# Layer 0 in two halves, one continuous dense stream, and a gated product of one ACT copy and three POOL products

## The chip, the cores and the metric

The kernel runs on one core of a Trainium2 chip. Its time is the device time in microseconds of one execution. Engines are named as the profile names them: PE multiplies matrices (PEld is its weight load), DVE, ACT and POOL work element by element, and SP issues most transfers. Each engine works through its own queue in order and waits at semaphores for the others. `V`, `S`, `G` and `T` in the code are DVE, ACT, POOL and PE.

## The reference, cut to what matters

All arrays are float32. Four batches of 512 tokens with 256 features pass two layers.

```python
xn = layernorm(x)                                     # layer 0
q, k, v = xn @ Wq.T + bq, xn @ Wk.T + bk, xn @ Wv.T + bv
context = (elu(q) + 1) * cumsum((elu(k) + 1) * v, axis=1) * 0.25
attn = context @ Wo.T + bo
xr = rms(xn) * norm_w                                 # and the gene part
vals, idx = top_k((xr @ Wc.T) / clip(temperature), 32)      # of 512
e = einsum(softmax(vals), genes[idx])
x = x + attn + tanh(e @ Wd.T) * xr * (e @ Wu.T) * scale

xn = layernorm(x)                                     # layer 1
q, k, v = split(rms(xn) @ w_qkv.T); w = exp(rms(k))
y = sigmoid(rms(q)) * cumsum(w * v) / (cumsum(w) + 1e-6)
u, g = split(y @ w_swiglu.T)                          # 2 x 1024 columns
dense = xn + (u * silu(g)) @ w_out.T
# 16 experts, the best 2 of each token (inner width 176), and a shared
# expert of inner width 352 that every token passes
x = x + dense + moe(xn) + shared_expert(xn)
```

## The kernel before

The tokens lie on the partitions in 16 tiles of 128, four to a batch; `xs` holds x throughout. Python generators describe pieces of work, `yield` marks places where another piece may come in, and `together` interleaves several generators in proportion to how far each has come. A tile scheduler then decides the final order within each engine's queue; tile pools with few buffers make a piece wait until an earlier user is done.

- `layer0(b, i0, nt)` does layer 0 for nt tiles: `statistics` (mean `mv`, inverse deviations `rs`; `sl` at L232 scales the logits), `normalise` (L213, one DVE instruction for a tile), transposes (L221), the logits (L289), the search for the 32 best of 512 (`top`: four rounds of an eight-fold maximum, L301, and a replacement, L302, on DVE, then the exponential L307), the linear attention (`attend_kv`, `attend_q`: projections L244, `phi` L257 to L259, a running sum L271 on DVE, the product with q into `ctxT` L280 on DVE with the factor 0.25 as `QSCALE`), the gene part (`express`, L316 to L334, whose last steps are POOL's `dn` and `xs` products) and the output projection (`out`, L339).
- `mix(b, i0, nt)` is layer 1 up to `yT`: statistics and `normalise` again, xs plus xn1 on POOL (L368), the w1 projections (L384), the copy of q and k (L391, ACT), the scaling of v (L393, DVE), squares (L396), roots, exponentials (L410, L411), the product with v on POOL (L412), transposes and running sums (L421), the reciprocal (L430), `yT` (L432), and the choice of experts (L439 to L456).
- `dense(b, half, busy)` takes 256 tokens through 11 chunks of 128 hidden columns, three of the shared expert (input `xn1T`) and eight of the swiglu (input `yT`). A chunk is an "up" (eight matmuls into the PSUM tile `gu`, L578), a tanh (L582, ACT), a gated product, and a "down" (four matmuls, L595, added up in `acc`) that comes two chunks later. `gu` has three buffers, `acc` one. Each half runs its own last two downs out before the next half's first up, and ends with acc added to xs (L614).
- `route`, `scatter`, the expert loop (pairs of 128-row groups: L738, L747, L759) and the final part: the gather of each token's two expert rows (L804, POOL) and their addition to xs (L815, DVE). `pr` (L486) is the first matmul of `route`.

The gated product of a chunk is

```python
V.scalar_tensor_tensor(th[0:m], th[0:m], 1.0, gu[0:m, 0], ALU.add, ALU.mult)
if busy:
    S.copy(hid[0:m], gu[0:m, 1])
    G.tensor_tensor(hid[0:m], hid[0:m], th[0:m], ALU.mult)
else:
    V.tensor_tensor(hid[0:m], gu[0:m, 1], th[0:m], ALU.mult)
```

with `busy` true for the four halves of batches 0 and 1, that is 44 of the 88 chunks. The order is: layer 0 of the first two tiles; mixing of these beside layer 0 of the other two; then the mixing of one batch, layer 0 of the next and one dense half together, three times; the mixing of batch 3 with the last half of batch 1, in which the expert weights are fetched into `wex` (after a memset of part of it on POOL); then routing and scattering beside 22 chunks of batch 2; the experts; and batch 3's 22 chunks beside the gathers and final additions. `paced` ties some transfers to the dense chunks' downs.

Of the kernel before, what the change touches and what calls it, by code (L numbers as in the profile page):

```python
# [11 lines left out]
F32 = mybir.dt.float32  # L12
# [4 lines left out]
P = 128  # L17
B, L, D = 4, 512, 256
NT = L // P
# [34 lines left out]
def tile_two_layers(  # L54
# [79 lines left out]
    nc.sync.dma_start(wot, wo0.rearrange("(h p) e -> p h e", p=P))  # L134

# [12 lines left out]
    for b in range(1, B):  # L148
        load_x(b)
# [5 lines left out]
    for h in range(NH):  # L155
        V.tensor_scalar(wct[:, h], wct[:, h], nwc[:, h : h + 1], None, ALU.mult)
    rtemp = wp.tile([P, 1], F32, name="rtemp")
# [28 lines left out]
    one = first.enter_context(tc.tile_pool(name="one0", bufs=1, side="right"))  # L186
# [7 lines left out]
    def statistics(pool, b, i0, nt):  # L194

        mv = pool.tile([P, NT, 2], F32, name="mv")
        rs = pool.tile([P, 2, NT], F32, name="rs")
        ve = pool.tile([P, NT], F32, name="ve")
        for i in range(nt):
            bs = pool.tile([P, 6], F32, name="bs")  # L200
            V.bn_stats(bs, xs[:, b, i0 + i])
            V.bn_aggr(mv[:, i], bs)
        V.tensor_scalar(rs[:, 0, 0:nt], mv[:, 0:nt, 1], LN_EPS, None, ALU.add)
        V.reciprocal(ve[:, 0:nt], rs[:, 0, 0:nt])
        V.tensor_tensor(ve[:, 0:nt], ve[:, 0:nt], mv[:, 0:nt, 1], ALU.mult)
        V.tensor_scalar(rs[:, 1, 0:nt], ve[:, 0:nt], RMS_EPS, None, ALU.add)
        S.activation(rs[:, :, 0:nt], rs[:, :, 0:nt], AF.Sqrt)
        V.reciprocal(rs[:, :, 0:nt], rs[:, :, 0:nt])
        return mv, rs

    def normalise(to, b, i0, nt, mv, rs):
        for i in range(nt):
            V.tensor_scalar(  # L213
                to[:, i], xs[:, b, i0 + i], mv[:, i, 0:1], rs[:, 0, i : i + 1], ALU.subtract, ALU.mult
            )
# [8 lines left out]
    def layer0(b, i0, nt):  # L224

        W = nt * P
        mv, rs = statistics(io, b, i0, nt)
        xn = io.tile([P, NT, D], F32, name="xn")
        normalise(xn, b, i0, nt, mv, rs)

        sl = io.tile([P, 2, NT], F32, name="sl")
        V.tensor_scalar(sl[:, 0, 0:nt], rs[:, 1, 0:nt], rtemp, None, ALU.mult)  # L232
        V.tensor_scalar(sl[:, 1, 0:nt], rs[:, 1, 0:nt], scl, None, ALU.mult)
        yield
        xnT = io.tile([P, NH, L], F32, name="xnT")
        for h in range(NH):
            S.copy(xnT[:, h, 0:W], turn(xn, nt, h * P))  # L237
        yield


        def project(c):
            pm = bank()[:, 0:W]
            for h in range(NH):
                T.matmul(  # L244
                    pm,
                    wqkv[:, h, c * P : (c + 1) * P],
                    xnT[:, h, 0:W],
                    start=(h == 0),
                    stop=(h == NH - 1),
                )  # L250
            return pm

        def phi(c):

            pm = project(c)
            e = io.tile([P, L], F32, name="phi", bufs=3)[:, 0:W]
            S.activation(e, pm, AF.Relu, bias=nbqk[:, c : c + 1], scale=-1.0)  # L257
            S.activation(e, e, AF.Exp, scale=-1.0)
            V.scalar_tensor_tensor(e, pm, bqkv1[:, c : c + 1], e, ALU.add, ALU.max)  # L259
            return e  # L260

        ctxT = one.tile([P, NH, L], F32, name="ctxT")
        cums = {}

        def attend_kv(h):
            fk = phi(2 + h)
            pv = project(4 + h)
            kv = one.tile([P, L], F32, name="kv")[:, 0:W]
            V.scalar_tensor_tensor(kv, pv, bqkv[:, 4 + h : 5 + h], fk, ALU.add, ALU.mult)
            cum = io.tile([P, L], F32, name="cum")[:, 0:W]  # L270
            V.tensor_tensor_scan(  # L271
                cum, ones[:, 0:W], kv, carry[:, h : h + 1] if i0 else 0.0, ALU.mult, ALU.add
            )
            if i0 + nt < NT:
                V.tensor_copy(carry[:, h : h + 1], cum[:, W - 1 : W])
            cums[h] = cum

        def attend_q(h):
            fq = phi(h)
            V.scalar_tensor_tensor(ctxT[:, h, 0:W], fq, QSCALE, cums[h], ALU.mult, ALU.mult)  # L280


        rden = io.tile([P, NT], F32, name="rden")
        exT = one.tile([P, L], F32, name="exT")

        def logits(i):
            pl = bank()
            for h in range(NH):
                T.matmul(  # L289
                    pl, xnT[:, h, i * P : (i + 1) * P], wct[:, h], start=(h == 0), stop=(h == NH - 1)  # L290
                )
            lg = io.tile([P, NG], F32, name="lg")
            S.copy(lg, pl)
            return lg

        def top(i, lg):
            tp = io.tile([P, NACT], F32, name="top")
            rep = io.tile([P, NG], F32, name="rep")
            for r in range(NACT // 8):
# [3 lines left out]
                if r == 0:  # L303
                    nm = io.tile([P, 1], F32, name="nm")
                    V.tensor_scalar(nm, tp[:, 0:1], sl[:, 0, i : i + 1], -1.0, ALU.mult, ALU.mult)
                    e = io.tile([P, NG], F32, name="e")
                    S.activation(e, lg, AF.Exp, bias=nm, scale=sl[:, 0, i : i + 1])  # L307
            den = io.tile([P, 1], F32, name="den")
            V.scalar_tensor_tensor(e, rep, TAKEN, e, ALU.is_equal, ALU.mult, accum_out=den)
            V.reciprocal(rden[:, i : i + 1], den)  # L310
            return e

        def express(i, e):
# [8 lines left out]
            S.copy(exT[:, i * P : (i + 1) * P], px[:, 0:P])  # L322
            du = bank()
            T.matmul(du, exT[:, i * P : (i + 1) * P], wdut, start=True, stop=True)  # L324
# [8 lines left out]
            G.tensor_tensor(xs[:, b, i0 + i], xs[:, b, i0 + i], bob, ALU.add)  # L333
            G.tensor_tensor(xs[:, b, i0 + i], xs[:, b, i0 + i], dn, ALU.add)  # L334

        def out(i):
# [5 lines left out]
            V.tensor_tensor(xs[:, b, i0 + i], ao, xs[:, b, i0 + i], ALU.add)  # L342


        parts = [lambda h=h, f=f: f(h) for h in range(NH) for f in (attend_kv, attend_q)]
        lg = logits(0)
        for i in range(nt):
            nxt = logits(i + 1) if i + 1 < nt else None
            e = top(i, lg)
            yield  # L350
            for part in parts[i * len(parts) // nt : (i + 1) * len(parts) // nt]:
                part()
            yield
            express(i, e)
            lg = nxt
            yield
        for i in range(nt):
            out(i)
            yield

    def mix(b, i0, nt):
# [17 lines left out]
        for i in range(nt):  # L379
# [13 lines left out]
            V.tensor_scalar(vs[:, i], pv[:, 0:D], rs[:, 1, i : i + 1], None, ALU.mult)  # L393
            for j in range(2):
                junk = w2.tile([P, D], F32, name="junk")
# [170 lines left out]
    def dense(b, half, busy):  # L566


        unit = (b, 2 * half) if (b, 2 * half) in made else (b, 0)
        t0 = (2 * half - unit[1]) * P  # L570
        ins = [a[:, :, t0 : t0 + HB] for a in made[unit]]
        acc = ps_a.tile([P, 2, D], F32, name="acc")

        def up(gw, g0, uw, u0, m, which, dw, dc):
# [6 lines left out]
            th = wd.tile([P, HB], F32, name="th", bufs=3)  # L581
            S.activation(th[0:m], gu[0:m, 0], AF.Tanh, scale=0.5)  # L582
            hid = wd.tile([P, HB], F32, name="hid", bufs=4)
            V.scalar_tensor_tensor(th[0:m], th[0:m], 1.0, gu[0:m, 0], ALU.add, ALU.mult)  # L584
            if busy:
                S.copy(hid[0:m], gu[0:m, 1])  # L586
                G.tensor_tensor(hid[0:m], hid[0:m], th[0:m], ALU.mult)  # L587
            else:
                V.tensor_tensor(hid[0:m], gu[0:m, 1], th[0:m], ALU.mult)  # L589
            return hid  # L590

        def down(n, hid):
            m, dw, dc = chunks[n][4], chunks[n][6], chunks[n][7]
            for t in range(2):
# [8 lines left out]
            beat.append(mm.ins.name)  # L603

        hids = []
        for n, c in enumerate(chunks):
            hids.append(up(*c))
            if n >= 2:
                down(n - 2, hids[n - 2])
            yield  # L610
        for n in (NC - 2, NC - 1):
            down(n, hids[n])
        here = xs[:, b, 2 * half : 2 * half + 2]
        V.tensor_tensor(here, acc, here, ALU.add)  # L614
        yield


    def chain(*parts):
        for part in parts:
            yield from part  # L620

    H = NC + 1

    def a(b, i0, nt):
        return layer0(b, i0, nt), 2 + 4 * nt

    def m(b, i0, nt):
        return mix(b, i0, nt), 6 + nt

    def d(b, half, busy=True):  # L630
        return dense(b, half, busy), H

    together(a(0, 0, 2))
    together(m(0, 0, 2), a(0, 2, 2))
# [5 lines left out]
    together(m(0, 2, 2), a(1, 0, 4), d(0, 0))  # L640
    together(m(1, 0, 4), a(2, 0, 4), d(0, 1))
    together(m(2, 0, 4), a(3, 0, 4), d(1, 0))
# [27 lines left out]
    together(m(3, 0, 4), d(1, 1), (load_experts(), 17))  # L670
    mixing.close()
    routing = ctx.enter_context(ExitStack())
    d2 = chain(dense(2, 0, False), dense(2, 1, False))
    together((route(), 8), (islice(d2, 6), 6))
    routing.close()

    together((scatter(), 33), (islice(d2, 15), 15))
    run_all(d2)
# [121 lines left out]
    for step, _ in enumerate(chain(dense(3, 0, False), dense(3, 1, False))):  # L800
# [11 lines left out]
        while added < 2 * NTT and 9 * added <= 16 * (step - 4):  # L812
# [61 lines left out]
```

## Time and profile before

| | |
|---|---|
| median of 10 runs | 591.61 us (589.47 to 593.33) |
| profiled execution, its own time | 592.26 us |
| its span, first to last instruction | 590.6 us |
| mean granted TensorE clock | 0.978 |
| busy: PE, DVE, ACT, POOL | 540.4, 375.1, 233.1, 171.9 us |
| busy share: PE, DVE, ACT, POOL | 92%, 64%, 39%, 29% |
| all transfers | 47.39 MB |

The profile names a group of instructions by line, engine, operation, and output and input tiles with their shape; after the bar stand the busy time in us and the mean of one in ns, then the idle time of the engine just before these instructions and what ended it. The rows of slices show 40 equal stretches of the span with the busy share of each engine in tenths. The table by stretches has, for each window, its bounds and length, each engine's busy time with the count of instructions in the order PE, PEld, DVE, ACT, POOL, and then the granted clock, the share of DMA and its rate in GB/s. The chain of waits follows the work that ended last back to the start; a row has the start in us, the length in us, the engine, tile and line. Matmuls are pipelined and their ends are modelled, so a busy PE is not always at its full pace.

### The profile page before, as it was taken

The page shows a single profiled execution, that of the slowest core. Times are in us where ns is not written, and L with a number is a line of the kernel's source. Part 1 is how long each engine was busy: PE and PEld are TensorE (multiplying, and loading weights), DVE is VectorE, ACT ScalarE, POOL GpSimd, SP SyncE. Part 2 cuts the span into 40 slices and gives each one's busy share as a digit, 9 for nine tenths or more (in the row PEclk, how much of TensorE's full clock was granted, in tenths as well). Part 3 has the DMA queues.
Part 4 walks back from the last instruction along what each step waited for, and adds up shares of the span by engine and source line. Part 5 has one row for each costly group of instructions (what it writes and reads, how often), then busy time and mean ns, then how long its engine had stood idle before and what let it go on. Part 6 is the DMA issues. An engine that isn't in the chain of part 4 may idle for free.

```text
span 590.6 us, 7339 instructions
## 1 busy us (share of the span) xinstructions
PE 540.4 (92%) x2384; PEld 393.9 (67%) x2384; DVE 375.1 (64%) x992; ACT 233.1 (39%) x528; POOL 171.9 (29%) x214
## 2 busy tenths in 40 slices
PE   3557989989999999999999999979999999999897
PEld 1333556567565776567767778866777777788686
DVE  3979999998796897968953795323222222235553
ACT  1453846652655716457155411112333333321011
POOL 1234232343222523224250325661000000016660
PEclk9788999999999999999999999989999999999899
DMA  5993000000000000000065702224333333124440
GB/s 160 374 376 139 1 1 0 2 0 1 1 1 0 0 2 1 1 1 0 2 187 156 233 13 71 96 83 142 94 105 105 108 108 98 55 68 129 125 143 28
DMA packets 38453, 47.39 MB, mean 80 GB/s; under 512 B 4016, under 2 KB 34960, under 8 KB 38160
## 3 DMA queue, kind: packets, MB, share of 16 engines
q1 hardware_dynamic: 35344, 38.53, 20.1%
q0 software_dynamic: 3072, 8.39, 4.6%
q8 instruction: 20, 0.33, 0.2%
q14 instruction: 17, 0.14, 0.1%
HBM read 28.30 MB, written 18.61 MB: 79 GB/s over the span
## 4 chain that ended last, share of the span: by engine, by line
PE 62%; DVE 24%; ACT 5%; issue 5%; POOL 2%; DMA 1%; SPq 0%; ACTq 0%; DVEq 0%
PE gu L578 17%; PE acc L595 10%; PE pu L738 9%; PE py L759 7%; PE pm L384 5%; PE pt L701 4%; DVE rep L302 3%; DVE top L301 3%; PE pm L244 3%; DVE sums L430 3%; PE pm L289 3%; DVE sums L421 2%; PE pm L324 2%; DVE xn L213 1%; PE pm L221 1%
## 5 line engine op out<-in xcount | busy, mean ns | idle before, releaser
L578 PE MATMUL gu<-yT,wugt 128*128 128x256 f32 x512 | 126.2, 383 | 0.0
L578 PEld LDWEIGHTS gu<-yT,wugt 128*128 128x128 f32 x512 | 95.8, 191 | 19.8 <-issue 7.4
L582 ACT ACTIVATE th<-gu 128x256 f32<-128x256 f32 (+1 forms) x88 | 33.2, 382 | 129.6 <-PE gu L578 88.6
L595 PE MATMUL acc<-wot,hid 128*128 128x256 f32 x256 | 68.1, 392 | 8.9 <-DVE hid L589 6.1
L804 POOL DMA_INDIRECT ys<-yrows,slot x32 | 30.5, 953 | 143.1 <-DMA yrows<-yg 127.6
L584 DVE SCALAR_TENSOR_TENSOR th<-th,gu 128x256 f32<-128x256 f32 (+1 forms) x88 | 36.0, 411 | 51.1 <-ACT th L582 28.9
L738 PE MATMUL pu<-wex,xgT 128*128 x188 | 63.8, 461 | 0.8 <-ACT xgT L715 0.8
L595 PEld LDWEIGHTS acc<-wot,hid 128*128 128x128 f32 x256 | 48.6, 194 | 20.8 <-DVE hid L589 7.7
L587 POOL TENSOR_TENSOR hid<-hid,th 128x256 f32<-128x256 f32 (+1 forms) x44 | 33.7, 769 | 95.7 <-ACT hid L586 95.6
L244 PE MATMUL pm<-xnT,wqkv 128*128 128x512 f32 (+1 forms) x120 | 46.4, 527 | 4.5 <-ACT qk L391 1.7
L747 DVE TENSOR_TENSOR hb<-pu,hb 128x176 f32<-128x176 f32 x47 | 16.1, 342 | 51.0 <-ACT hb L746 51.0
L578 PE MATMUL gu<-xn1T,sgu 128*128 128x256 f32 (+1 forms) x192 | 45.9, 384 | 0.0
L384 PE MATMUL pm<-w,xn1T 128*128 128x512 f32 (+1 forms) x128 | 44.8, 493 | 0.6 <-DVE vs L393 0.6
L759 PE MATMUL py<-wex,hgT 128*128 x188 | 44.5, 379 | 0.0
L759 PEld LDWEIGHTS py<-wex,hgT 128*128 128x128 f32 x188 | 35.6, 190 | 8.6 <-issue 0.2
L578 PEld LDWEIGHTS gu<-xn1T,sgu 128*128 128x128 f32 (+1 forms) x192 | 34.7, 184 | 7.0 <-issue 0.9
L738 PEld LDWEIGHTS pu<-wex,xgT 128*128 128x128 f32 x188 | 32.0, 190 | 11.0 <-ACT xgT L715 1.0
L384 PEld LDWEIGHTS pm<-w,xn1T 128*128 128x128 f32 x128 | 24.2, 190 | 22.2 <-issue 17.7
L244 PEld LDWEIGHTS pm<-xnT,wqkv 128*128 128x128 f32 x120 | 23.8, 201 | 22.3 <-issue 13.9
L751 DVE COPY hgT<-pt 128x512 f32<-128x512 f32 (+1 forms) x24 | 16.3, 681 | 34.3 <-PE pt L701 34.3
L544 POOL DMA_INDIRECT xrows<-xn,slot x32 | 30.9, 966 | 23.1 <-DVE cpair L538 9.7
L289 PE MATMUL pm<-wct,xnT 128*128 128x512 f32 x64 | 33.7, 666 | 0.3 <-ACT xnT L237 0.2
(162 smaller groups left out, 880.6 us busy)
## 6 DMA issues: line engine op xcount, KB each, us to landing
xrows<-zero SPq DMA_DIRECT2D x1, 6016.0 KB, 22.6
xg<-xrows SPq DMA_DIRECT2D x23, 256.0 KB, 4.2
yrows<-yg SPq DMA_DIRECT2D x23, 256.0 KB, 2.1
wex<-in_w_gate_up_dram SPq DMA_DIRECT2D x8, 704.0 KB
xs<-in_x_dram SPq DMA_DIRECT2D x4, 512.0 KB
wugt<-in_wug_dram SPq DMA_DIRECT2D x1, 2048.0 KB, 12.1
wex<-in_w_down_dram SPq DMA_DIRECT2D x4, 512.0 KB
out_dram<-xs SPq DMA_DIRECT2D x7, 256.0 KB, 2.8
```

Of the source, the lines that this page charges most:

```text
L244: T.matmul(pm, wqkv[:, h, c * P : (c + 1) * P], xnT[:, h, 0:W], start=(h == 0), stop=(h == NH - 1),)
L289: T.matmul(pl, xnT[:, h, i * P : (i + 1) * P], wct[:, h], start=(h == 0), stop=(h == NH - 1))
L384: T.matmul(o[:, 0:n], xnT[:, h, i * P : (i + 1) * P], w1[:, h, at : at + n], start=(h == 0), stop=(h == NH - 1),)
L544: sc = G.indirect_dma_start(out=xrows, out_offset=bass.IndirectOffsetOnAxis(ap=slot[:, k, i : i + 1], axis=0), in_=xn1[:, i // NT, i % NT] ...
L578: T.matmul(gu[0:m, k], w[:, h, at : at + m], ins[which][:, h], start=(h == 0), stop=(h == NH - 1))
L582: S.activation(th[0:m], gu[0:m, 0], AF.Tanh, scale=0.5)
L584: V.scalar_tensor_tensor(th[0:m], th[0:m], 1.0, gu[0:m, 0], ALU.add, ALU.mult)
L587: G.tensor_tensor(hid[0:m], hid[0:m], th[0:m], ALU.mult)
L595: mm = T.matmul(acc[:, t], hid[0:m, t * P : (t + 1) * P], dw[0:m, dc], start=(n == 0 and t == 0), stop=(n == NC - 1), skip_group_check=True,)
L738: T.matmul(pg[:, 0 : 2 * NI], xT[:, i, h], wex[:, bass.ds(at[i] + h * 2 * NI, 2 * NI)], start=(h == 0), stop=(h == NH - 1),)
L759: mm = T.matmul(py[:, i * D : (i + 1) * D], hT[:, i, h], wex[:, bass.ds(at[i] + EW - (2 - h) * D, D)], start=(h == 0), stop=(h == 1),)
L804: G.indirect_dma_start(out=ys[:, asked], out_offset=None, in_=yrows, in_offset=bass.IndirectOffsetOnAxis(ap=slot[:, k, n : n + 1], axis=0) ...
```

## The change

Layer 0 is split into `front` (statistics, normalising, transposes, the four tiles' logits and the attention, always for a whole batch) and `back` (search, gene part and output projection for nt tiles). In `front` the product into `ctxT` is made by POOL; the factor 0.25 goes into `wot` once, by an ACT instruction. For batches 0 and 1 (`wide`) the projections use the PSUM tiles of the dense part. `normalise` and the scaling of v become ACT instructions; for that, `statistics` gets one more small DVE instruction, which forms minus mean times inverse deviation. The logits' exponential is written in place and `lg` has five buffers.

`dense` becomes one stream of 88 chunks through all eight halves, in which downs stay two chunks behind across the meeting of two halves; `islice(dd, n)` takes the next n. While `calm` is empty (all mixing) a chunk's product is made without DVE: an ACT copy of both halves of `gu`, and three POOL products, gate·up, tanh times that, and the sum. From `route` on, DVE makes the product as it did before. `th` has two buffers instead of three, `junk` one instead of two. 40 chunks lie in the mixing now, 26 in routing and scattering, 22 at the end. The order of work is written anew, x of batch 1 is fetched ahead of the layer 1 weights, and the final additions follow the chunks by another rule.

```diff
+    load_x(1)
     w1 = const.tile([P, NH, 3 * D + NE], F32, name="w1")
...
+    S.mul(wot, wot, QSCALE)
...
         V.reciprocal(rs[:, :, 0:nt], rs[:, :, 0:nt])
+        V.scalar_tensor_tensor(mv[:, 0:nt, 0], mv[:, 0:nt, 0], -1.0, rs[:, 0, 0:nt], ALU.mult, ALU.mult)
...
-            V.tensor_scalar(
-                to[:, i], xs[:, b, i0 + i], mv[:, i, 0:1], rs[:, 0, i : i + 1], ALU.subtract, ALU.mult
+            S.activation(
+                to[:, i], xs[:, b, i0 + i], AF.Identity, bias=mv[:, i, 0:1], scale=rs[:, 0, i : i + 1]
             )
...
-    def layer0(b, i0, nt):
+    def front(b, wide):
...
         def project(c):
-            pm = bank()[:, 0:W]
+            if wide:
+                pm = ps_d.tile([P, 2, HB], F32, name="gu").rearrange("p i c -> p (i c)")
+            else:
+                pm = bank()
...
-            V.scalar_tensor_tensor(ctxT[:, h, 0:W], fq, QSCALE, cums[h], ALU.mult, ALU.mult)
+            G.tensor_tensor(ctxT[:, h], fq, cums[h], ALU.mult)
...
+        for h in range(NH):
+            for i in (2 * h, 2 * h + 1):
+                logits(i)
+                yield
+            attend_kv(h)
+            yield
+            attend_q(h)
+            yield
+
+    def back(b, i0, nt):
...
+        top(i0)
+        yield
+        for i in range(i0, i0 + nt):
+            if i + 1 < i0 + nt:
+                top(i + 1)
+                yield
+            express(i)
             yield
-        for i in range(nt):
+        for i in range(i0, i0 + nt):
             out(i)
             yield
...
-            V.tensor_scalar(vs[:, i], pv[:, 0:D], rs[:, 1, i : i + 1], None, ALU.mult)
+            S.activation(vs[:, i], pv[:, 0:D], AF.Identity, scale=rs[:, 1, i : i + 1])
...
-            th = wd.tile([P, HB], F32, name="th", bufs=3)
+            th = wd.tile([P, HB], F32, name="th", bufs=2)
             S.activation(th[0:m], gu[0:m, 0], AF.Tanh, scale=0.5)
             hid = wd.tile([P, HB], F32, name="hid", bufs=4)
-            V.scalar_tensor_tensor(th[0:m], th[0:m], 1.0, gu[0:m, 0], ALU.add, ALU.mult)
-            if busy:
-                S.copy(hid[0:m], gu[0:m, 1])
-                G.tensor_tensor(hid[0:m], hid[0:m], th[0:m], ALU.mult)
+            if spare:
+                V.scalar_tensor_tensor(th[0:m], th[0:m], 1.0, gu[0:m, 0], ALU.add, ALU.mult)
+                V.tensor_tensor(hid[0:m], gu[0:m, 1], th[0:m], ALU.mult)
             else:
-                V.tensor_tensor(hid[0:m], gu[0:m, 1], th[0:m], ALU.mult)
+                both = w2.tile([P, 2, HB], F32, name="both")
+                S.copy(both[0:m], gu[0:m])
+                G.tensor_tensor(hid[0:m], both[0:m, 0], both[0:m, 1], ALU.mult)
+                G.tensor_tensor(th[0:m], th[0:m], hid[0:m], ALU.mult)
+                G.tensor_tensor(hid[0:m], hid[0:m], th[0:m], ALU.add)
...
+        behind = []
+        for half in range(2 * B):
...
+            for n, c in enumerate(chunks):
+                behind.append((half, n, up(ins, bool(calm), *c)))
+                if len(behind) > 2:
+                    down(*behind.pop(0))
+                yield
...
+    f0, f1 = front(0, True), front(1, True)
+    b0 = back(0, 0, 2)
+    run_all(islice(f0, 4))
+    together(some(f0, 6), some(b0, 2))
+    together(some(b0, 4), some(f1, 2))
+    m0 = mix(0, 0, 2)
+    next(m0)
+    run_all(islice(f1, 3))
+    together((m0, 7), some(f1, 5))
...
-    together(m(0, 2, 2), a(1, 0, 4), d(0, 0))
-    together(m(1, 0, 4), a(2, 0, 4), d(0, 1))
-    together(m(2, 0, 4), a(3, 0, 4), d(1, 0))
+    together((back(0, 2, 2), 6), d(3))
+    m0 = mix(0, 2, 2)
+    next(m0)
+    run_all(islice(dd, 2))
+    together((m0, 7), d(3))
+    together((back(1, 0, NT), 12), (front(2, False), 10), d(9))
+    m1 = mix(1, 0, NT)
+    next(m1)
+    run_all(islice(dd, 2))
+    together((m1, 9), (back(2, 0, NT), 12), (front(3, False), 10), d(3))
+    m2 = mix(2, 0, NT)
+    next(m2)
+    run_all(islice(dd, 2))
+    together((m2, 9), (back(3, 0, NT), 12), d(9))
...
-    together(m(3, 0, 4), d(1, 1), (load_experts(), 17))
+    m3 = mix(3, 0, NT)
+    next(m3)
+    run_all(islice(dd, 2))
+    together((m3, 9), d(5), (load_experts(), 17))
...
-    together((route(), 8), (islice(d2, 6), 6))
+    calm.append(True)
+    together((route(), 8), d(5))
...
-    together((scatter(), 33), (islice(d2, 15), 15))
-    run_all(d2)
+    together((scatter(), 33), d(15))
+
+    run_all(islice(dd, 6))
...
-        while added < 2 * NTT and 9 * added <= 16 * (step - 4):
+        while added < 2 * NTT and 17 * added <= 32 * (step - 3):
```

## The prediction, made before the changed kernel was run

> **What bounds the kernel now.** I read the page's slices first, then the table by stretches, the chain of waits for the pace of the matmuls, the groups by form for prices, and last who waits for whom.
>
> From the page, tenths of 40 slices of 14.8 us:
>
> ```profile
> PE   3557989989999999999999999979999999999897
> DVE  3979999998796897968953795323222222235553
> PEclk9788999999999999999999999989999999999899
> ```
>
> PE is full from slice 6 on; DVE is full before that and nearly full until slice 19; the clock is granted in part only where PE starves. The table by stretches (length, then busy time of PE, PEld, DVE, ACT, POOL):
>
> ```profile
> 0.00:80.00 80.00, 50.86 (x193) 30.70 (x194) 65.83 (x210) 35.92 (x79) 21.62 (x37) 0.89 0.56 194
> 80.00:140.00 60.00, 56.81 (x243) 36.02 (x244) 58.16 (x161) 32.38 (x69) 23.68 (x33) 1.00 0.00 1
> 140.00:220.00 80.00, 78.04 (x343) 53.37 (x341) 66.27 (x165) 40.87 (x92) 23.96 (x30) 1.00 0.00 1
> 220.00:290.00 70.00, 67.78 (x294) 44.45 (x294) 58.16 (x155) 39.12 (x87) 21.80 (x26) 1.00 0.00 1
> 346.00:406.00 60.00, 55.65 (x248) 47.21 (x246) 26.04 (x69) 7.67 (x20) 32.67 (x37) 0.97 0.23 78
> ```
>
> Matmuls overlap, so busy time flatters PE. The chain of waits shows their real pace where nothing holds them:
>
> ```profile
> 169.11 1.72 PE pm L289 x4
> 170.83 2.63 PE pm L384 x8
> 414.69 1.73 PE py L759 x8
> 419.67 1.73 PE py L759 x8
> 531.08 1.73 PE gu L578 x8
> 533.67 1.73 PE gu L578 x8
> ```
>
> A 512-column matmul (two records) takes 0.86 us, a dense chunk 2.59 (up 1.73, down 0.86), an expert pair 4.97. So 88 chunks are 228 us, 23.5 pairs 117, layer 0 of a batch 28.5 (logits 6.9, projections 10.4, expression 6.9, out 3.5, transposes 0.9; four times 114), the mixing of a batch 14.0 (56 in all): 515 us. The span is 590.6, so PE loses 75. Counting records at that pace by stretch, the losses are 41 (to 80 us), 5 (to 140), 8 (to 290), 3 (to 346), 8 (to 406), 1 (experts), 9 (end, of it 4 at 550 to 557 where two halves of the dense part meet, and 4 to 5 of tail). The PE work is the same matmuls in both kernels; only these 75 us can move.
>
> **The change, part by part.** Prices, from the groups by form (mean ns after the comma):
>
> ```profile
> L584 DVE SCALAR_TENSOR_TENSOR th<-th,gu 128x256 f32<-128x256 f32 x80 | 32.8, 412 | 48.7 <-ACT th L582 27.4 <-issue 21.1
> L587 POOL TENSOR_TENSOR hid<-hid,th 128x256 f32<-128x256 f32 x40 | 30.8, 774 | 86.1 <-ACT hid L586 86.1
> L586 ACT COPY hid<-gu 128x256 f32<-128x256 f32 x40 | 14.9, 372 | 35.7 <-DVE th L584 35.5
> L391 ACT COPY qk<-pm 128x512 f32<-128x512 f32 x16 | 9.3, 582 | 20.2 <-PE pm L384 20.2
> L213 DVE TENSOR_SCALAR xn<-xs,mv,rs 128x256 f32<-128x256 f32 x32 | 15.2, 526 | 0.2
> ```
>
> *DVE.* Leaves: the dense product, 44 of L584 (18.1 us); 32 normalisations (16.8); 16 of L393 (476 ns, 7.6); ten ctxT products (5.8); the doubled fixed cost of batch 0's halves (about 2). Comes: ten small products of mv (0.2 each, 2). Some 48 us less.
>
> *ACT.* The dense copy goes from 372 to 582 ns (same shape as L391): 40 times 0.21 is 8.4 us. A normalisation with two pointer operands has no row: without pointers a 256-wide pass from SBUF takes 413 (L258), with one 509 (L410), and two pointers add 185 at 512 wide (L307's 813 against 628); so 0.41 to 0.60, and I take 0.55, as it has two: 17.6 us. The vs product has a like row, 473 (L326): 7.6. The listing of the changed kernel's ACT queue has 29 table loads where 23 stood, at 1283 each: 7.7. Together 41 us; ACT goes from 53% of 80 to 290 to about two thirds.
>
> *POOL.* A chunk goes from one product to three. Its row has median 727, mean 774: 40 times 1.5 is 60 us, and eight ctxT products at about 1.33 (L368, 512 wide) add 11. POOL goes from 33% to some 60%.
>
> *The start.* Both listings have the same searches (32 MAX8, 32 replacements) in DVE's queue between the first MAX8 and the last yT of batch 0. By row means the items between sum to 137.0 us before and 114.7 after; before, they took 125.2 (15.3 to 140.5). At that ratio, 0.914, they take 105 after. The first MAX8 comes some 2 us later (ACT normalises four tiles in 2.2 us before the transposes, where DVE did the first two in 0.7), so this point falls at 122. The PE work queued up to there is about 89, against 94.5 in the trace: 33 lost instead of 46, if nothing else waits. But I then walked the queues instruction by instruction and found waits that the old order lacks: a ctxT product ahead of the second chunk's last product on POOL (2 us to PE), the second half's statistics behind a search on DVE (PE out of chunks for 3.5), three table loads between w1's last matmul and the exponentials (1.5 to 5). By the walk the point falls at 133 with 91 done: 42 lost. I take a gain of 6, between 4 and 13. The moved load of x (0.5 MB ahead of the layer 1 weights on SP's queue) delays these by 1.4 us at the 376 GB/s of that stretch; w1 is first used at 51 us, 20 us after it lands, so it costs nothing, and 1.4 if that cover were gone. The new scaling of wot on ACT stands ahead of the second logits copy and waits for a transfer issued at 11.8 (bob beside it took 6.2): up to 1 us, hidden by DVE's first search.
>
> *The middle, 140 to 346.* DVE was at 83% of 140 to 290, PE lost 11. Relief there is worth little: the waits of PE for DVE in 80 to 346 sum to 6 us. The new chain of a chunk is tanh 0.38, copy 0.58, three products 2.2, with hand-overs about 3.6 us, against the 4.3 us of the two next ups and a down that PE has meanwhile: hidden by 0.7. Its waits come where something stands ahead: the xs+xn1 product (2.4), the memset of wex (3.5) and dn products on POOL, four normalisations ahead of a copy on ACT. Walking the mixing of batch 1 gives 6 us lost where the trace lost 4, that of batch 3 also 6 where it lost 3. I add 4, between minus 6 (DVE relief wins) and plus 16 (third rival).
>
> *The scatter, 346 to 406.* Route, 32 scatters at 1.27 us and the first fetch last 60 us there, and 22 chunks (57 us) stand beside them in both. The 8 lost belong to one wait of ACT (8.7 us at 381, put down to no instruction). I leave it: 0, down to minus 6 if it does not recur.
>
> *The end.* One stream puts the next half's ups where PE waited: of 4 lost I count 3 back; the final additions move one chunk (2.6 us) nearer to their gathers, so 0 to minus 4.
>
> Sum: -6 +4 +0 -3 = -5. The profiled run took 592.26, 1.7 outside its span; the median is 591.61. From the median: 586.5.
>
> **A rule against it.** The row: DVE's sl<-rs of 128x4 (L232) has min 216, median 224, max 686 ns; the longest ones lie beside POOL products, while the POOL product itself has min 718 and median 726. The Trainium skill, "SBUF — State Buffer", section "SBUF: two separate sides", says that POOL and a DVE instruction with two SBUF inputs or in a two-port mode lock each other out for the whole instruction. By the rule some 100 such DVE instructions would meet a POOL at 60% and wait half a product, an estimate of 22 us of DVE time, which would leave half of DVE's relief; by the row only the few small ones pay about 0.46, 5 or so for each of five mixing chains, 11 us, of which the 4 above holds what is exposed.
>
> **Rivals.** *POOL becomes the bound (slower).* Each chunk's three products stand in one in-order queue with dn, vs, ctxT, xs and the memset; where one product or more stands ahead, the chain passes 4.3 us and PE's acc waits for POOL, as it did four times (2.4 us) with a single product. It decides from a chain 0.7 us longer on: if 20 of the 40 chunks pay one product, 0.73, it is 15 instead of 4 less, and 591.6 -9 +19 gives 601. For it: eight times the POOL work on the chain of a down matmul; against it: two chunks of cover and POOL idle 40%.
> *The start pays in full (much faster).* 13 there, the middle -1, the ACT wait gone half, end 4: 574. For it DVE's full slices 2 to 9, against it the walk.
> *DVE's relief is off the path (no change).* PE's work is unchanged and full from 122 on; what the start gains, ACT's extra loads take: 591.6.
>
> **How the numbers follow.** Forecast 0.50 (own range 580 to 592), POOL bound 0.30 (594 to 610), start in full 0.12 (568 to 580), no change 0.08. From 574 to 602 leaves out a good third of the POOL case and half of the third: 0.18. A measurement here tells about 0.2%, 1.2 us. Faster takes 0.45 of the forecast and the third case: 0.57; within 0.2%, 0.09; slower 0.34.
>
> **What would show it.** Right: DVE busy about 48 less, POOL about 70 more; the first yT later than before's 79 us (about 90) but PE further at 130 us; gu<-yT without a gap at the meeting of the last halves; PE's waits for POOL hid under 8 us. Wrong: those waits at 15 or more, DVE busy falling by less than 30 (lock-out), or PE still losing over 46 by 140 us.

## The result and the profile after

The changed kernel takes 600.79 us (median of 9 runs, 597.50 to 602.35) beside 591.8 us of the kernel before (median of 31): a ratio of 1.0144 (95% interval 1.0126 to 1.0161), 9 us slower. The forecast was 5 us faster. The profiled execution has a span of 600.5 us. PE's work is what it was; PE now loses 85 us of the span where it lost 75.

Three rows of the page's slices (tenths, 15.0 us a slice):

```profile
PE   3949979899999989999899499879999999999997
DVE  2899998289673849924842982322222222225563
POOL 1332058386747172666783027650000000006661
```

PE's slices 2 and 4 are fuller than they were (slice 3 has 4 where it had 5) and DVE has holes from slice 8 on, so the relief came. But in slice 23 (330 to 345 us), where PE was full, stands a 4, and POOL shows a 0 just there: PE starves while POOL is idle. The table by stretches shows the same place; first after (columns as in the prediction), then before in the last two windows:

```profile
0.00:80.00 80.00, 56.81 (x159) 26.99 (x160) 66.60 (x214) 51.96 (x92) 20.43 (x35) 0.95 0.57 194
80.00:140.00 60.00, 57.33 (x259) 39.88 (x260) 45.01 (x122) 37.51 (x78) 38.84 (x53) 0.95 0.00 1
326.00:350.00 24.00, 15.29 (x70) 11.84 (x69) 18.40 (x25) 5.06 (x13) 5.22 (x11) 0.86 0.32 94
350.00:410.00 60.00, 53.53 (x224) 44.73 (x223) 23.14 (x62) 7.08 (x19) 31.00 (x32) 0.91 0.26 88
```

```profile
326.00:350.00 24.00, 22.55 (x112) 18.38 (x111) 19.62 (x29) 7.65 (x21) 8.62 (x16) 1.00 0.47 147
350.00:410.00 60.00, 54.79 (x244) 45.88 (x243) 23.84 (x63) 9.86 (x23) 30.92 (x32) 0.97 0.27 93
```

Between 326 and 350 us PE did 70 matmul records instead of 112. The timeline of after tells why; each row has start, length, engine and line, and in brackets the idle time before it and what ended it (three DVE rows, one of PE, one of POOL):

```profile
338.96 3.36 DVE L435 RECIPROCAL sums<-sums 128x256 f32<-128x256 f32 x2
342.23 1.16 DVE L426 TENSOR_TENSOR_SCAN sums<-ones,pm 128x512 f32<-128x512 f32 x1
343.31 0.39 DVE L590 SCALAR_TENSOR_TENSOR th<-th,gu 128x256 f32<-128x256 f32 x1
```

```profile
344.69 1.22 PE L606 MATMUL acc<-wot,hid 128*128 128x256 f32 x2 [8.02 <-DVE hid L591]
```

```profile
344.45 0.20 POOL L472 MEMSET stri<- 128x128 f32 x1 [14.01 <-DVE yT L437]
```

This is the end of batch 3's mixing: running sums and reciprocals on DVE, one after the other. The chunk that PE waits for belongs to the routing, so its product is made by DVE (L590, L591). Its tanh was ready at 334.5 us; its DVE instruction stands in the queue behind two pairs of reciprocals and starts at 343.31. The 7 chunks planned beside this mixing (11 before) were used up by then. POOL, which could have made the product, was idle for 14.0 us.

The second place is the scatter. The chain of waits of after:

```profile
376.52 2.39 issue
378.92 2.02 PE acc L606 x4
...
390.66 8.44 another core or an unknown queue
399.11 0.39 ACT th L587
399.53 0.43 DVE th L590
399.99 0.43 DVE hid L591
```

ACT sits 8.44 us before a tanh whose matmuls are in the trace at their usual times. The semaphore by which PE signals finished matmuls explains it: one update reaches the others at 371.21, the next at 377.54, then four at once between 380.36 and 380.61; again nothing from 393.45 to 399.09, then five within 0.3 us. PE's signals are **late** there, and the granted clock is 0.63 from 378 to 382 and 0.69 from 398 to 402 us. Before has this too; between 350 and 420 us 13.4 us of its ACT's waits are put down to no instruction ("remote"; a row of waits has the us in total, how many, and the longest):

```profile
ACT th L582 <- remote: 13.4, 3, 8.7
```

It comes at the end of the kernel as well, beside POOL's 32 gathers. In before the first of two tanh starts 2.7 us after its eight matmuls have ended:

```profile
546.47 1.89 PE L578 MATMUL gu<-yT,wugt 128*128 128x256 f32 x8
551.04 0.66 ACT L582 ACTIVATE th<-gu 128x256 f32<-128x256 f32 x2 [4.86 <-PE gu L578]
```

PE's losses, counted as in the prediction from the matmul records at their unhindered pace; in the last column, whether signals come late between 350 and 425 us by PE's semaphore:

| kernel | 0–140 | 140–326 | 326–350 | 350–425 | rest | span | late |
|---|---|---|---|---|---|---|---|
| before | 46.0 | 8.6 | 2.8 | 8.7 | 8.6 | 590.6 | yes |
| after | 40.1 | 13.1 | 11.9 | 13.5 | 6.0 | 600.5 | yes |
| e14, more chunks | 38.8 | 13.1 | 2.8 | 16.1 | 6.1 | 592.8 | yes |
| e15, no scatters | 40.1 | 13.1 | 12.1 | 1.7 | 6.8 | 589.7 | no |
| e10, after | 40.5 | 13.2 | 12.1 | 1.7 | 5.1 | 588.5 | no |
| e11, more chunks | 40.5 | 13.4 | 2.6 | 8.5 | 5.3 | 586.2 | no |
| e17, e11 and two of batch 3 | 39.2 | 12.9 | 2.8 | 1.5 | 6.3 | 578.6 | no |

After against before: start -5.9, middle +4.5, end of the last mixing +9.1, scatter +4.8, end -2.6; together +9.9, the difference of the spans. (After's scatter varies: by the same count it loses about 11 us in e5 and e13.)

### The profile page after: what moved, and what is told of

It reads as the page before. It is cut to its first block, busy times and chain, and to the rows that moved or that the text cites. A ratio compares the mean times of both kernels' runs of the same rounds, so it can differ in the third digit from the quotient of the medians.

```text
span 600.5 us, 7343 instructions
## 1 busy us (share of the span) xinstructions
PE 546.3 (91%) x2360; PEld 391.2 (65%) x2360; DVE 342.8 (57%) x890; ACT 266.0 (44%) x568; POOL 236.4 (39%) x298
## 4 chain that ended last, share of the span: by engine, by line
PE 56%; DVE 25%; ACT 7%; POOL 4%; issue 3%; DMA 2%; another core or an unknown queue 1%; SPq 0%; DVEq 0%; POOLq 0%; ACTq 0%
PE gu L583 15%; PE pu L770 9%; PE acc L606 8%; PE py L791 7%; PE pm L389 5%; DVE rep L312 4%; DVE top L311 4%; PE pt L733 3%; DVE sums L435 3%; DVE sums L426 2%; PE pm L283 2%; PE pm L224 2%; PE pm L334 1%; DMA wqkv<-in_wqkv_dram 1%
## 5 line engine op out<-in xcount | busy, mean ns | idle before, releaser
L606 PE MATMUL acc<-wot,hid 128*128 128x256 f32 x256 | 70.7, 395 | 14.3 <-DVE hid L591 11.9
L583 PE MATMUL gu<-xn1T,sgu 128*128 128x256 f32 (+1 forms) x192 | 50.2, 398 | 0.1
L590 DVE SCALAR_TENSOR_TENSOR th<-th,gu 128x256 f32<-128x256 f32 (+1 forms) x48 | 20.0, 417 | 50.9 <-ACT th L587 32.6
L779 DVE TENSOR_TENSOR hb<-pu,hb 128x176 f32<-128x176 f32 x47 | 16.1, 342 | 51.0 <-ACT hb L778 51.0
L595 POOL TENSOR_TENSOR hid<-both 128x256 f32<-128x256 f32 (+1 forms) x40 | 29.8, 746 | 33.4 <-ACT both L594 33.3
L583 PEld LDWEIGHTS gu<-xn1T,sgu 128*128 128x128 f32 (+1 forms) x192 | 36.1, 193 | 9.5 <-issue 2.6
L311 DVE MAX8 top<-rep 128x8 f32<-128x512 f32 x48 | 32.7, 681 | 0.3
L312 DVE MATCH_REPLACE8 rep<-top,rep 128x512 f32<-128x512 f32 x48 | 32.3, 674 | 0.0
```

The source lines that it names most:

```text
L311: V.max(tp[:, 8 * r : 8 * r + 8], src)
L312: V.match_replace(rep, tp[:, 8 * r : 8 * r + 8], src, TAKEN)
L583: T.matmul(gu[0:m, k], w[:, h, at : at + m], ins[which][:, h], start=(h == 0), stop=(h == NH - 1))
L595: G.tensor_tensor(hid[0:m], both[0:m, 0], both[0:m, 1], ALU.mult)
L606: mm = T.matmul(acc[:, t], hid[0:m, t * P : (t + 1) * P], dw[0:m, dc], start=(n == 0 and t == 0), stop=(n == NC - 1), skip_group_check=True,)
```

## The experiments

Kernels of one set ran on one chip, beside runs of before. Before takes 591 to 592 us in the first result and in sets 2 and 4, where PE's signals come late in the scatter, and 587 us in sets 1, 3 and 5, where no trace shows that. What differs between these groups is not known. The record numbers the chips of sets 1 to 5 as 6, 14, 0, 9 and 9: set 4, with late signals, and set 5, without them, bear the same number, so unless it stands for two chips, the chip alone does not decide it. So ratios are compared within a group.

**Set 1: chunks, or POOL?** (before 587.06)

e1, four chunks moved from the scatter to the last mixing:

```diff
-    together((m3, 9), d(5), (load_experts(), 17))
+    together((m3, 9), d(9), (load_experts(), 17))
-    together((scatter(), 33), d(15))
+    together((scatter(), 33), d(11))
```

> Theory T: the loss sits at the end of batch 3's mixing, where the dense chunks planned beside it run out and the next chunk's DVE product stands behind the reciprocals. With 9 chunks asked for beside that mixing instead of 5, and 11 instead of 15 in the scatter, the wait of PE for DVE's hid falls from 8.0 us to under 3, PE loses about 4 us between 326 and 350 us instead of 11, and the time falls by 7 to 10 us, to about 592. Rival R (POOL's three products are the bound): four more three-product chunks give POOL 9 us more work on the chain, waits of PE for POOL's hid appear, and the time stays at 599 or above.

587.42 us, ratio 1.0007 (0.9996 to 1.0018). The 8 us wait is gone; PE loses 2.8 us in 326 to 350. POOL's four added chunks cost no wait. But after itself is at 589.94 in this group (e10 below), so the gain is 2.5 us and not 7 to 10.

e2, the same counts, but the routing's chunks made by ACT and POOL (`both` in a pool of its own):

```diff
-    calm.append(True)
     together((route(), 8), d(5))
     routing.close()
+    calm.append(True)
...
```

> The same number of chunks everywhere, but the five chunks of the routing are formed by ACT and POOL too, so no DVE product stands behind the reciprocals of batch 3. Theory T: the 8.0 us wait goes, POOL (idle from 330 to 344 us in the trace of after) takes the products, and the time falls by 6 to 9 us, to about 593. If the shortage is of chunks alone and not of DVE, the wait only changes its name and the time falls by under 3. Rival R: the wait turns into one for POOL's hid and the time stays at 599 or above.

586.71 us, 0.9995 (0.9984 to 1.0007). With not one chunk more in the plan the wait is gone as well (2.8 us lost): DVE's queue, not the number of chunks alone, made it. In both, a new wait came up behind it, of PE for the first rows of the experts (e1):

```profile
PE pt L733 <- DMA xg<-xrows: 4.7, 1, 4.7
```

e3, the changed order with the old product in the mixing:

```diff
-                both = w2.tile([P, 2, HB], F32, name="both")
-                S.copy(both[0:m], gu[0:m])
-                G.tensor_tensor(hid[0:m], both[0:m, 0], both[0:m, 1], ALU.mult)
-                G.tensor_tensor(th[0:m], th[0:m], hid[0:m], ALU.mult)
-                G.tensor_tensor(hid[0:m], hid[0:m], th[0:m], ALU.add)
+                V.scalar_tensor_tensor(th[0:m], th[0:m], 1.0, gu[0:m, 0], ALU.add, ALU.mult)
+                S.copy(hid[0:m], gu[0:m, 1])
+                G.tensor_tensor(hid[0:m], hid[0:m], th[0:m], ALU.mult)
```

> The changed kernel, with the 40 mixing chunks formed as in the kernel before (DVE sum-product, ACT copy of 256, one POOL product). Theory T: DVE is busy about 16 us more and POOL 60 less, the middle (80 to 290 us) loses within 3 us of what it loses in after, the tail's 8 us wait stays; time 598 to 604. Rival R: the three products were the cost, the time falls to 593 or below.

597.80 us, 1.0189 (1.0171 to 1.0208). After itself is 1.0045 in this group (e10), so the old product costs 1.4%, 8 us, in the new order: PE loses 21.6 instead of 13.2 us in 140 to 326. The expectation put the middle within 3 us and was wrong there. PE's longest waits, from 290 us on:

```profile
PE gu L583 <- ACT hid L594: 11.8, 2, 7.9
```

ACT's copy stands behind DVE's product, and that behind reciprocals. Of the two waits only the one of 3.9 us, at 300 us, lies in the middle and is new; the one of 7.9 ends at 346.7 us and is the wait of the last mixing, which after has too. The rest of the loss in the middle is in shorter waits.

e4, the old order with three POOL products:

```diff
-            V.scalar_tensor_tensor(th[0:m], th[0:m], 1.0, gu[0:m, 0], ALU.add, ALU.mult)
             if busy:
-                S.copy(hid[0:m], gu[0:m, 1])
-                G.tensor_tensor(hid[0:m], hid[0:m], th[0:m], ALU.mult)
+                both = w2.tile([P, 2, HB], F32, name="both")
...
+                G.tensor_tensor(hid[0:m], hid[0:m], th[0:m], ALU.add)
```

> The kernel before, with its 44 mixing chunks formed by the ACT copy and three POOL products (th with two buffers and junk with one, as in after, to make room). Theory T: the chunk's form by itself costs nothing that counts, 589 to 595, with waits of PE for POOL's hid under 6 us. Rival R: it costs most of the 9 us, 598 or above, with 8 us and more of waits for POOL's hid.

592.78 us, 1.0105 (1.0083 to 1.0127). The time itself lies in the range of theory T, but before takes 587.06 in this set, so the form costs 6 us, between the two expectations. PE's waits for POOL of this kernel:

```profile
PE acc L598 <- POOL hid L589: 4.4, 5, 1.3
PE pm L221 <- POOL vs L412: 4.2, 5, 1.5
```

The waits for POOL's hid rose from 2.4 to 4.4 us, as the POOL rival said but under the 6 us of theory T. More of it is vs (4.2 where before had 0.2), which the three products hold up in POOL's queue and which the running sums need: the last yT ends at 349.7 us, in the first trace of before at 345.3.

**Set 2: again, and two more** (before 591.37)

> The changed kernel, unchanged, for a second profile beside the other runs. In its first profile PE's signals came late twice between 370 and 406 us, for all engines at once, with 11.5 us lost; e1 to e4 show no such stall. If the stalls belong to the kernel, they are there again, and the ratio to before is 1.0144 again. If they belong to the execution or the chip, they are gone here, the wait of 8 us for DVE's hid at 337 us stays, and the ratio is what the tail alone makes, 1.002 to 1.016, by how many stalls before loses too.

600.94 us, 1.0172 (1.0145 to 1.0200): late signals again, 8.3 us lost between 370 and 390 alone.

> The kernel before, unchanged, for a second profile. Its first profile has one such stall (381 to 391 us, 8 us lost between 350 and 406). If the stall is of the execution, PE loses under 4 us there, or else the 4 to 5 us reappear as a wait for the first xg, since the scatter ends late in any case.

590.31 us, 0.9984 (0.9964 to 1.0004): late signals in before again, 8.8 us lost between 350 and 425.

e7, e2 with two chunks moved from ahead of the last mixing to the scatter (`d(9)` to `d(7)` beside `back(3)`, `d(15)` to `d(17)`):

> e2 with two chunks moved from the layer 0 of batch 3 to the scatter (9 to 7, 15 to 17). In e2 PE waits 4.6 us for the first xg and was full before the routing. Theory T: the routing then starts 4 to 5 us earlier, the wait for xg falls below 1, and the time is 4 to 5 us under e2, a ratio to before of 0.990 to 0.994. If the mixing of batch 3 is bound by its own chain and not by PE's queue, the routing starts no earlier, PE loses the 5 us in the mixing instead, and the ratio stays at 0.998 to 1.001.

605.31 us, 1.0228 (1.0198 to 1.0258). The theory failed: the routing starts at 347.3 us, 344.5 in e2. The last mixing is bound by its own chain, and with two chunks fewer PE loses 8.9 us at its end; with the late signals it loses some 19 more between 350 and 425 us.

e8, e1 with e3's product:

> e1 (9 chunks beside the last mixing, 11 in the scatter), with the mixing chunks formed as before (DVE, ACT, one POOL product). Theory T: every chunk of the last mixing now has a DVE product that queues behind running sums and reciprocals, so the three-product form is worth something here: 3 to 8 us more than e1, a ratio of 1.006 to 1.014. If the form does not matter once enough chunks are there, the ratio is that of e1, 0.999 to 1.003. If POOL was the cost, it is below 0.997.

603.42 us, 1.0194 (1.0165 to 1.0223), against 1.0075 of e14 in the same group: with enough chunks the old product costs 1.2%, 7 us. The last yT ends at 351.2, in e14 at 343.1.

**Set 3: one chip without late signals** (before 587.27)

e9, before with the dense part as one stream (as in after, old product) and the later additions:

> The kernel before with one of the changes alone: the dense part as one continuous stream of 88 chunks (downs two chunks behind across the meeting of halves, 11 chunks where a half stood, so 6, 15 and 1 in routing, scatter and after it) and the later rule for the final additions. My sum put the end at 3 us: if it holds, the wait of 4 us at 550 to 557 us goes and the ratio is 0.993 to 0.997. If the end is bound by the gathers, the same time comes back as a longer tail, 0.999 to 1.002.

586.63 us, 0.9990 (0.9977 to 1.0003): nothing. PE waits 5.2 us for the first xg here, which may be where the gain of the end went; no trace of before without late signals was kept, so this is not shown.

> The changed kernel once more, on the same chip as e11 and e12, so that these can be compared with it directly. 1.0126 to 1.020 to before if the chip makes PE's late signals in the scatter; 1.004 to 1.012 if it does not.

589.94 us, 1.0045 (1.0029 to 1.0061). Without late signals the change costs 2.7 us, not 9.

> e1 again (9 chunks beside batch 3's mixing, 11 in the scatter), on one chip with after. Theory T: 8 to 10 us less than after, 1.3 to 1.7 of its per cent, of them 8 from the wait for DVE's hid, if the stalls are as many in both. If what e1 gained was only the chip without stalls, it is within 3 us of after.

587.05 us, 0.9994 (0.9983 to 1.0004): 2.9 us less than after. PE loses 9.5 less at 326 to 350, but 6.8 more by 425: it now arrives early and waits 4.7 us for xg.

> e2 again (the routing's five chunks formed by ACT and POOL, counts as in after), on one chip with after. Theory T: as e11, 7 to 10 us less than after. If the number of chunks were the cause and not DVE's queue, within 3 us of after.

587.03 us, 1.0003 (0.9990 to 1.0016), as e11. Both fell short of the 7 to 10 us that I expected of them here.

**Set 4: one chip with late signals** (before 592.25)

> The changed kernel as the base of this set. By the two profiles with late signals (PE's signals reach the other engines 3 to 6 us late, twice in the scatter) it is 1.0126 to 1.020 to before, and PE loses 9 to 12 us between 350 and 410 us; without them 1.003 to 1.006 and under 2 us.

600.59 us, 1.0134 (1.0112 to 1.0156), late signals as expected.

> e1 again, beside after on this chip. With late signals: theory T (the tail's 8 us wait and the late signals add up, since PE is never ahead of the scatter in after) gives 8 to 10 us less than after, 0.999 to 1.003 to before; the rival, that the late signals come with the changed order of the work and hit e1 as they hit after, gives 1.008 or more. Without late signals: as e11, 0.998 to 1.001.

595.30 us, 1.0075 (1.0046 to 1.0104): 5.3 us less than after, of a gap of 8.3 to before. The tail's wait is gone, but the late signals take more, 16.1 us of PE's time in 350 to 425 where after loses 13.5 and before 8.7. So neither expectation holds alone.

e15, after without the scatters (the experts then see none of the tokens):

```diff
-                sc = G.indirect_dma_start(
...
-                paced(sc)
                 yield
```

> after without the 32 scatters (xrows keeps its zeros, so the experts see none of the tokens; all other work is the same). If the late signals need the scatters' transfers, PE runs 346 to 406 us without a loss, under 2 us, and on a chip with late signals the time falls by 8 to 12 us against after; if they come from PE's own load, the loss stays. On a chip without late signals the time is within 3 us of after, since PE and not the scatter sets the end of that part in after.

591.49 us, 0.9982 (0.9965 to 0.9998): 9.1 us less than after. ACT's waits of this kernel between 350 and 420 us contain none put down to no instruction:

```profile
ACT th L578 <- PE gu L574: 51.9, 22, 5.4
```

In this stretch the late signals come with the scatters. At the end, beside the 32 gathers, e15 still has one: an up ends at 549.5 us and its tanh starts at 552.15. That the scatters' order or pace could avoid them was not tried.

e16, e1 with two chunks of batch 3 ahead of the experts:

```diff
-    run_all(islice(dd, 6))
+    run_all(islice(dd, 8))
-        while added < 2 * NTT and 17 * added <= 32 * (step - 3):
+        while added < 2 * NTT and 16 * added <= 32 * (step - 3):
```

> e1 with two chunks of batch 3 taken ahead of the experts (8 after the scatter instead of 6, 20 at the end instead of 22; the final additions' rule 16 instead of 17, so that all fit). In e1 PE waits 4.7 us for the first xg. Theory: where it does, these two chunks fill the wait and the time is 3 to 5 us under e1, 0.992 to 0.995 to before. If the gathers and not PE set the end, the tail grows by what the wait shrinks, and it is within 1 us of e1. With late signals PE has no such wait and the time is that of e14, within 2 us.

596.89 us, 1.0081 (1.0060 to 1.0102), as e14: the late signals leave no wait to fill.

**Set 5: the wait for xg** (before 587.29)

> e16 again. On the chip of e13 to e16 the late signals filled the wait for xg that the two chunks were meant for, and it was no faster than e14. If this run meets a chip without late signals, the wait of 4.7 us goes and the time is 0.992 to 0.996 of before; with late signals it is 1.006 to 1.010 again.

580.96 us, 0.9894 (0.9878 to 0.9910). This beats both kernels, 6 us under before and under e11. The window 350 to 410 in e11 and then in e17:

```profile
350.00:410.00 60.00, 54.55 (x242) 45.47 (x240) 23.45 (x62) 9.99 (x23) 30.85 (x32) 0.94 0.29 97
```

```profile
350.00:410.00 60.00, 59.04 (x273) 50.04 (x273) 25.02 (x67) 11.98 (x28) 30.91 (x32) 1.00 0.31 101
```

PE is full and the clock stays at 1.00; in e11 it was 0.50 from 402 to 406 us, just behind the wait, so the wait had also cost clock.

e18, the same two lines in e9 (`dd, 1` to `dd, 3`, 17 to 16):

> e9 (before with the continuous stream) with two chunks of batch 3 ahead of the experts (3 after the scatter instead of 1) and the final additions' rule at 16. In e9 PE waits 5.2 us for the first xg. Without late signals: that wait goes, 3 to 5 us under e9, 0.991 to 0.995 to before. With late signals: within 2 us of before.

582.09 us, 0.9913 (0.9897 to 0.9930). The two chunks are worth 1.0% in the new order (e11 to e17) and 0.8% in the old (e9 to e18). So most of e17's lead over before is theirs and not the change's: e18, with the old order and the old product, comes within 1.1 us of e17, and the two intervals overlap. By the count of the table, e18 loses 5.8 us more than e17 by 140 us, 5.0 less from 140 to 326 and 1.7 more at the end of the last mixing: what layer 0 in two halves gained at the start, the middle gave back.

## Why the prediction was wrong, step by step

*The start (-6): right.* PE loses 40.1 instead of 46.0 us by 140 us; first yT at 85.3, not 90.

*The middle (+4): right in the number up to 326 us, +4.5, wrong behind it.* Up to 326 us the number owes something to luck: the walk looked for waits behind POOL's queue and ACT's copies, but of PE's listed waits from 140 to 326 us, 6.4 us in all, 5.1 are for DVE, 1.3 for ACT and none for POOL. (Before's waits for DVE from 80 to 346 us, which the prediction puts at 6 us, are 5.0 in the list.) The step that failed is the sentence on batch 3's mixing, "that of batch 3 also 6 where it lost 3". It lost 11.9 where before lost 2.8, from 326 to 350 alone. So up to 350 us the middle lost 13.6 us more than before where the sum has 4. I walked that mixing as if each of its chunks had a POOL product, and took the 7 chunks planned there as enough. The scheduler draws the routing's chunks forward when these are used up, and those have DVE's product. e2 shows it with that product alone changed, e1 with the count alone.

*The scatter (0): wrong.* I left the wait without a name as it was, down to minus 6 and never above zero. It belongs to the scatters (e15), it differs between the sets, and it cost 4.8 us more in after, nearly all the rest of the miss. A wait whose cause I did not know deserved a bound on both sides.

*The end (-3): right as a loss of PE (-2.6), not as time.* e9 has this part alone and gains 0.6 us. The cause is also in doubt: at 548 to 551 us, just ahead of the 4 us that the prediction gives to the meeting of two halves, before has the late signal shown above, so part of these 4 may be the signal's.

*The sum itself.* I added up PE's losses as if each were time. But the experts start at the later of two things: PE's dense work, or the chain from the last yT through routing and 32 scatters, 57 to 60 us in e1, e2 and e9, where PE waits for its end. The last yT ends at 345.3 before and 344.3 after: what the start gained, the middle gave back. So in e11 the repaired tail's 9.5 us become 2.9 of time, because PE then waits for xg; e17 and e18 fill that wait, and there the gain of the repair appears, though the order as a whole stays within 1.1 us of the old one.

*POOL becomes the bound (601): right number, wrong cause.* The measured 600.79 lies inside the stated 574 to 602 only because this rival stretched the range; that is luck. PE's list of waits in after contains none for POOL's hid, and e3 and e8 show that this form saves 7 to 8 us in the new order. In the old order it costs 6 (e4), and there POOL's queue is the cause, through vs more than through hid.

*Engines.* POOL rose by 64 us (about 70 forecast) and ACT by 33 (41); a normalisation on ACT takes 590 ns, near the upper bound of 0.60. DVE fell by 32 instead of 48. Most of the gap lies in the counting: the prediction added up mean lengths, and added up in this way DVE's records fell by 41.4 us (425.9 to 384.5), while busy time counts records that overlap only once. Of the other 6.6, 3.3 are a miscount: 40, not 44, sum-products left, and four products came. About 3 us are left, in which small instructions that became longer show: cf<-rden,sl of 128x1 went from 333 to 453 ns, cwall of 128x64 from 206 to 562, while the maximum over 512 stays at 681 (686 before). The trace agrees with the lock-out that the Trainium skill, "SBUF — State Buffer", section "SBUF: two separate sides", describes: of the 16 cf<-rden,sl of after, 12 last 248 to 984 ns, and each of these ends 12 to 17 ns behind the POOL product beside which it began. But what it can have taken from DVE's relief on balance is these 3 us, not the 11 from the row or the 22 estimated by the rule. No experiment isolated it.

## What to carry to other kernels

Lost time of the fullest engine adds up only along one chain: before summing, find the events that all streams must pass (here the first rows for the experts) and ask for each which side comes last. When filler work is moved, count it at every place where the main chain runs alone on another engine, and look which engine forms the filler that the scheduler will draw in next. What a form of an operation costs is a property of the queue it stands in: three POOL products cost 6 us in one order and saved 8 in another.

## What the runs showed of the hardware

In the first result and in sets 2 and 4 PE's completion signals reached the other engines late and then in a burst, only while POOL's indirect transfers ran beside full PE work. Beside the 32 scatters the tanh of four ups starts 6 to 8 us after the up has ended in the traces of before and after; beside the 32 gathers at the end it is 2.7 us in before and 2.6 in e15. In the traces of sets 1, 3 and 5 no tanh behind 350 us starts more than 0.8 us after both its up and ACT's work ahead of it. The two groups differ by 4 to 5 us for before (587 to 592 us) and by 11 for after (590 to 601). Without the scatters the stretch from 350 to 425 us is free of it (e15), and after's time falls to 591.49. What delays the signals, and what differs between the groups, stays open.
